# A convolutional row LSTM: the shared third's normalisation on ScalarE, and another order for the half-step

## The chip, the cores and the metric

The kernel runs on one core of a Trainium2 chip. The metric is the device time of one execution in microseconds (us); the time of a kernel is the median of several executions. A core has a matrix engine (TensorE; PE in the profile, with its weight loads as PEld), VectorE (DVE), ScalarE (ACT), GpSimd (POOL), SyncE (SP), which issues the DMAs here, an on-chip memory SBUF and the accumulators PSUM, in which eight banks are used in turn.

## The reference

The input `x` has 8 images of 96 channels and 128 x 128 pixels. It is normalised in 32 groups, and goes through a row LSTM, whose result is added to `x`:

```python
its = conv(X, W_is * mask, 1x3) + b_is        # gates' own input, for all rows
def step(carry, row_in):                      # 128 rows, one after the other
    h, c = carry
    ss = conv(h, W_ss, 3 taps) + b_ss         # 96 -> 384 channels
    gates = ss + row_in                       # f, i, o, g of 32 channels each, three times
    f, i, o, g = sigmoid, sigmoid, sigmoid, tanh
    c_new = f * c + i * g
    h_new = o * tanh(c_new)
    return (h_new, c_new), h_new
x = x + rows(scan(step, groupnorm(x)))
```

Each row needs the state of the row above, so the 128 rows are a chain. The mask of the input's convolution lets the first third of the output channels see the first third of the inputs at the centre tap, the second third two, and the third all.

## The kernel before

**Two chains.** The images are split into two sets of four, s = 0 and s = 1. They share nothing but the weights, so a row of one can be worked while the other waits. A *half-step* is one row of one set; half-step n has row n // 2 of set n % 2, with set 0 one row ahead. There are 256.

**A half-step.** Pixels are held as even and odd ones, 256 of each kind (4 images x 64). The three-tap convolution of a row is taken from four operands, which are made from the new state `hx`: the sum `vs` of even and odd neighbours (S, `total`, L670), their difference `vf` (F, `difference`, L674), and the differences of shifted pixels `te` (D0, `shifted_even`, L680) and `vo` (D1, `shifted_odd`, L684). S and F are VectorE's, D0 and D1 GpSimd's. The products with them are called 1 (`vs`), 2 (`vf`), 0 (`vo`) and 3 (`te`); P, Q and E are those with the row's own input `xs`. Each is made for three tiles A, B and C of 128 gate channels, in one PSUM bank a tile; TensorE works in two lanes of 64 rows, marked `<` and `>`, and all its matmuls are L512.

When a tile's products are there, the two results must be combined: cp (`copy`, L583, ScalarE) brings one half to SBUF, lo (`even`, L587) and hi (`odd`, L591, both VectorE) add and subtract. Then come the gates: ta (tanh, L596), si (sigmoid, L615) and o2 (the last third of the output gate, L618), all on ScalarE; fg (`forget`, f x c, L623, VectorE); gt (i x g, of the odd pixels on VectorE, gtb, L632, of the even on GpSimd, gta, L630); ce (`cell`, L642, VectorE), th (`cell_tanh`, L650, ScalarE), ou (`output`, L658, VectorE, which writes the state `hx`). The letter a or b at a name's end is for the even and odd pixels, a capital for the tile. re (`residual`, L700, VectorE) adds the row to `x`.

**The input's preparation.** The rows are worked in blocks of R = 4, 32 of them. Each half-step also prepares a piece of a later block: W1 (`widen`, L337, GpSimd) normalises 128 x 512 pixels of one image from `xr` to `xw`; W2 (`add_pixels`, L354) and W3 (`subtract_pixels`, L358, both GpSimd) make from it two kinds of operand in `xs`. The channels of the last third, of which there is a copy beside the state (`hx<-x`, 32 partitions), are normalised by `normalise_shared`: mostly in pieces of 32 x 512 or 32 x 384, called U (L337, GpSimd), and once in four rows a piece of 32 x 128, called X (L335, ScalarE). `prepare(n, which)` issues those that `which` names, and with the last of them also the block's DMAs (`load_rows`, `load`, `spare`).

**The order.** The queues are written out by hand. `PERIOD` is a string of names that is issued for each of the half-steps 2 to 253, `LAST` for the end. The order of names within an engine is the order of its queue; between engines only semaphores count. A stroke `'` after a name means the half-step before, `+` the one after; S, F, D0 and D1 count from the row that will use them. So `PERIOD` is a loop over which the steps of several half-steps are spread, and `hiC` to `hiC` is a whole turn. Read by engine, one turn of the string before is:

- VectorE: fg' loB hiB loA gtb' hiA ceb' cea' oub' oua' F' S' loC hiC re'
- ScalarE: siA' cpB siBb' cpA taCb' taCa' siC' o2' thb' X tha' cpC taA siBa
- GpSimd: D0 U W3 D1 W1 gta' W2

Of the kernel before, what the change touches and what calls it, by code (L numbers as in the profile page):

```python
# [21 lines left out]
def kernel(  # L22
# [29 lines left out]
    nc = tc.nc  # L52
# [423 lines left out]
    class HalfStep:  # L476
# [158 lines left out]
        def part(self, ap, lo, hi, t=None):  # L635
            ap = ap.rearrange("p (t b j) -> p t b j", t=2, b=BH)
            return ap[:, :, lo:hi] if t is None else ap[:, t, lo:hi]
# [106 lines left out]
    def work(n):  # L744
        row, s = place(n)
        if row >= NT:
            return [], (), []
        if n < len(FIRST):
            return FIRST[n]
        k, r = divmod(row, R)  # L750
        ahead, image = (k + 2, 0) if r == R - 1 else (k + 1, r + 1)
        return (
            shared(s, k + 1, *SHARED[r]) if k + 1 < NB else [],
            own(s, ahead, image) if ahead < NB else (),
            ([LATER[n]] if n in LATER else [])
            + ([(spare, s, k + 1)] if r == R - 2 and k + 1 < NB else [])
            + ([(load_rows, s, k + 2)] + ([(load, 0, k + 2)] if s == 1 else [])
               if r == R - 2 and k + 2 < NB else []),
        )
# [3 lines left out]
    def prepare(n, which="123"):  # L763

        channels, image, rest = worked.setdefault(n, [list(parts) for parts in work(n)])
        now = []
        for name, engine in (("X", nc.scalar), ("U", nc.gpsimd)):
            if name in which:
                now += [part for part in channels if part[1] is engine]
                channels[:] = [part for part in channels if part[1] is not engine]  # L770
        for i in "123":
            if i in which and int(i) <= len(image) and image[int(i) - 1]:
                now.append(image[int(i) - 1])
                image[int(i) - 1] = None
        if image.count(None) == len(image) and n not in closed:
            closed.add(n)
            now += rest
        for part, *args in now:
            part(*args)
# [3 lines left out]
    def finish(n):  # L783
        prepare(n)
        row, s = place(n)
        k, r = divmod(row, R)
        if r == R - 1:
            store(s, k, R - 1 if k + 1 == NB else 0, R)
            if s == 1 and k + 2 < NB:
                load(s, k + 2)  # L790
        elif r == R - 2 and k + 1 == NB:
            store(s, k, 0, R - 1)
# [2 lines left out]


    PERIOD = (
        "2B> siA' cpB 2A< siBb' 0C'> 1A< cpA fg' D0'' 3C'> QC< loB QA+> taCb' 1C< hiB PB+> 2C< "
# [3 lines left out]
    )  # L802
    LAST = (
        "2B'' 2A'' 1B'' 1A'' cpB'' cpA'' loB'' 1C'' hiB'' 2C'' loA'' EB'' hiA'' 0B'' 3A'' 0A'' "
        "3B'' cpC'' loC'' EA'' taA'' hiC'' 0C'' 3C'' PA QA PB QB PC QC EA EB siBa'' siA'' siBb'' "
        "fg'' taCb'' taCa'' gtb'' siC'' gta'' ceb'' cea'' o2'' thb'' oub'' tha'' oua'' F'' S'' "
        "D1'' D0'' re'' 1A 2A 1B 1C 2B 2C cpA loA hiA cpB loB 3A hiB 0A 0B 3B cpC loC hiC 0C 3C "
        "taA siA fg o2 siBa siBb taCa taCb gta gtb siC ceb cea thb tha oub oua reb rea"
    )
# [17 lines left out]
    def do(n, names, by_lanes=False):  # L827

        for name in names.split():
            if name in "UX":  # L830
                prepare(n - NH, name)
                continue
            if name[0] == "W":
                prepare(n - 1 + name.count("+") - name.count("'"), name.strip("W+'"))
                continue
# [280 lines left out]
    for b in range(B):  # L1116
# [7 lines left out]
        for k in range(QW // CH):  # L1124
# [11 lines left out]
            if alone:  # L1136
                i = list(shares).index(k)
                part = slice(0, alone * SN) if k % 2 else slice(CH - alone * SN, CH)
# [131 lines left out]
```

## Time and profile before

| | |
|---|---|
| median of 3 runs | 2147.67 us (2146.77 to 2148.72) |
| the profiled execution | 2147.14 us |
| its span | 2145.3 us |
| granted TensorE clock | 0.995 |
| busy: PE, PEld | 2044.4 us (95%), 1727.8 us (81%) |
| busy: DVE, ACT, POOL | 1841.4 us (86%), 1584.9 us (74%), 1581.3 us (74%) |
| instructions on DVE, ACT, POOL | 4018, 3519, 1917 |
| U on GpSimd (L337, both shapes) | 245 instructions, 205.8 us |
| X and the like on ScalarE (L335) | 74 instructions, 39.9 us |
| DMA | 242.79 MB, 113 GB/s |

A row of a group (by line, engine, operation and shapes) ends with `| busy us, mean ns of one | idle time of the engine before them`. A row of the chain that ended last has start, length, engine, tile written and line. A row of a timeline has start, length, engine, line, operation, output `<-` inputs, shape, and in brackets the idle time just ahead and what ended it. A row of windows has the stretch, its length, the busy time of PE, PEld, DVE, ACT and POOL, the granted clock, the share of DMA time and GB/s. Times are counted from the start of the span.

### The profile page before, as it was taken

The numbers are of one execution on the slowest core, as the hardware profiler recorded it, in microseconds if no ns is written. First come the engines' busy times: TensorE is split into PE (matmuls) and PEld (weight loads), VectorE is DVE, ScalarE is ACT, GpSimd is POOL, SyncE is SP. The second block draws the span as 40 slices with busy tenths as digits, with TensorE's granted clock in tenths as the row PEclk, the third lists the DMA queues.
The fourth block names the chain that finished last, engine by engine and source line by source line (L and its number), as shares of the span: only waits on it lengthen the run. The fifth ranks groups of instructions, "written<-read, shape, count | busy, mean of one in ns | idle before, by whom it ended". The sixth has DMA issues, their size and how long they took to land.

```text
span 2145.3 us, 45095 instructions
## 1 busy us (share of the span) xinstructions
PE 2044.4 (95%) x16400; PEld 1727.8 (81%) x16400; DVE 1841.4 (86%) x4018; ACT 1584.9 (74%) x3519; POOL 1581.3 (74%) x1917
## 2 busy tenths in 40 slices
PE   3689999999999999999999999999999999999998
PEld 0357888888888888888888888888888888888886
DVE  5788888888888888888888888888888888888887
ACT  6687777777777777777777777777777777777776
POOL 4457877777777777777777777777777777777752
PEclk9989999999999999999999999999999999999999
DMA  9973443343344334334433433443343344334311
GB/s 404 412 222 94 99 109 82 95 114 100 84 102 107 84 95 114 99 83 103 107 83 95 114 98 83 104 107 83 95 114 98 83 105 106 83 95 114 92 35 31
DMA packets 110286, 242.79 MB, mean 113 GB/s; under 512 B 6832, under 2 KB 16368, under 8 KB 104048
## 3 DMA queue, kind: packets, MB, share of 16 engines
q1 hardware_dynamic: 110064, 239.89, 42.0%
q8 instruction: 131, 2.15, 0.4%
q14 instruction: 91, 0.75, 0.1%
HBM read 181.34 MB, written 50.33 MB: 108 GB/s over the span
## 4 chain that ended last, share of the span: by engine, by line
DVE 53%; ACT 21%; PE 18%; issue 4%; DMA 2%; POOL 2%; SPq 0%; DVEq 0%; POOLq 0%; ACTq 0%
PE ps L512 18%; DVE ps L591 12%; DVE ps L587 11%; DVE vs L670 9%; ACT ps L650 7%; DVE c L642 7%; ACT m L583 6%; DVE hx L658 5%; DVE vf L674 5%; DVE g L632 3%; ACT g L596 2%; ACT o L618 2%; DMA xs<-in_x_dram 2%; ACT o L615 2%; ACT hx L335 1%
## 5 line engine op out<-in xcount | busy, mean ns | idle before, releaser
L512 PE MATMUL ps<-vo,wl 64*128 64x256 f32 (+1 forms) x3042 | 815.3, 392 | 27.3 <-DVE ps L591 2.1
L512 PE MATMUL ps<-vs,wm 64*128 64x256 f32 (+1 forms) x3046 | 808.2, 397 | 8.4 <-POOL vs L670 6.0
L512 PE MATMUL ps<-vf,wm 64*128 64x256 f32 (+1 forms) x3046 | 794.9, 385 | 3.2 <-DVE vf L674 1.8
L512 PE MATMUL ps<-te,wl 64*128 64x256 f32 (+1 forms) x3042 | 771.7, 377 | 0.0
L512 PE MATMUL ps<-xs,wx 64*128 64x256 f32 (+1 forms) x3080 | 727.7, 377 | 2.0 <-POOL xs L354 1.8
L512 PEld LDWEIGHTS ps<-xs,wx 64*128 64x128 f32 x3080 | 561.4, 187 | 7.4 <-POOL xs L354 3.4
L512 PEld LDWEIGHTS ps<-vo,wl 64*128 64x128 f32 (+1 forms) x3042 | 421.3, 185 | 163.3 <-DVE ps L591 129.4
L512 PEld LDWEIGHTS ps<-vf,wm 64*128 64x128 f32 (+1 forms) x3046 | 492.7, 186 | 71.5 <-DVE vf L674 29.2
L583 ACT ACTIVATE m<-ps,wl 128x256 f32<-128x256 f32 x766 | 363.1, 474 | 235.1 <-PE ps L512 208.9
L596 ACT ACTIVATE g<-ps 32x512 f32<-32x512 f32 x765 | 317.9, 448 | 254.4 <-PE ps L512 247.9
L512 PEld LDWEIGHTS ps<-te,wl 64*128 64x128 f32 (+1 forms) x3042 | 493.0, 187 | 13.3 <-issue 0.2
L512 PEld LDWEIGHTS ps<-vs,wm 64*128 64x128 f32 (+1 forms) x3046 | 424.9, 186 | 67.3 <-DVE vs L670 40.8
L680 POOL TENSOR_TENSOR te<-hx 96x256 f32<-96x256 f32 x254 | 215.4, 848 | 292.8 <-DVE hx L658 290.8
L587 DVE TENSOR_TENSOR ps<-m,ps 128x256 f32<-128x256 f32 x768 | 324.7, 423 | 82.4 <-ACT m L583 82.0
L358 POOL TENSOR_TENSOR xs<-xw 128x512 f32<-128x512 f32 (+1 forms) x254 | 380.5, 1498 | 20.2
L591 DVE TENSOR_TENSOR ps<-m,ps 128x256 f32<-128x256 f32 x768 | 325.8, 425 | 17.6
L658 DVE TENSOR_TENSOR hx<-o,ps 96x256 f32<-96x256 f32 x512 | 197.4, 415 | 130.0 <-ACT ps L650 129.5
L512 PE MATMUL ps<-xs,wt 64*128 64x256 f32 x1012 | 299.4, 376 | 1.5 <-DVE ps L591 1.5
L630 POOL TENSOR_TENSOR g<-i,g 96x256 f32<-96x256 f32 x251 | 182.6, 727 | 123.9 <-ACT g L596 123.9
L615 ACT ACTIVATE ps<-ps 96x512 f32<-96x512 f32 (+1 forms) x512 | 244.0, 477 | 0.2
L700 DVE TENSOR_TENSOR x<-x,hx 96x512 f32<-96x512 f32 x253 | 232.2, 918 | 0.0
L337 POOL TENSOR_SCALAR hx<-x,rstd,nmr 32x512 f32<-32x512 f32 (+1 forms) x245 | 205.8, 840 | 24.7
(118 smaller groups left out, 2524.4 us busy)
## 6 DMA issues: line engine op xcount, KB each, us to landing
xr<-in_x_dram SPq DMA_DIRECT2D x124, 512.0 KB, 6.4
x<-in_x_dram SPq DMA_DIRECT2D x62, 768.0 KB, 5.9
out_dram<-x SPq DMA_DIRECT2D x62, 768.0 KB, 4.7
xs<-in_x_dram SPq DMA_DIRECT2D x31, 1024.0 KB, 11.2
x<-in_x_dram SPq DMA_DIRECT2D x62, 256.0 KB, 3.2
te<-in_x_dram SPq DMA_DIRECT2D x8, 1024.0 KB, 11.3
hx<-in_x_dram SPq DMA_DIRECT2D x8, 1024.0 KB, 9.7
te<-xs SPq DMA_DIRECT2D x62, 128.0 KB, 2.5
```

The costliest lines, as they stand in the source:

```text
L337: return engine.tensor_scalar(dst, src, scale, shift, ALU.mult, ALU.add)
L358: return engine.tensor_sub(differences, strided(xw[:, 0, :], 0, [(W + 1, n), (J + 1, 2), (1, J)]), strided(xw[:, 0, :], J, [(W + 1, n), (0 ...
L512: made = nc.tensor.matmul(self.ps[a][:, bass.ts(half, HB)][:, cols], weights[rows, bass.ts(a, P)], rhs[rows, cols], start=new, stop=False, ...
L583: nc.scalar.activation(self.m1[a], m1, AF.Identity, bias=column)
L587: nc.vector.tensor_add(self.ps[a][:, 0:HB], self.m1[a], self.ps[a][:, HB:])
L591: nc.vector.tensor_sub(hi, self.m1[a], hi)
L596: nc.scalar.activation(self.part(g, lo, hi, t), self.part(ps, lo, hi, t), AF.Tanh)
L615: nc.scalar.activation(to, gate, AF.Sigmoid)
L658: nc.vector.tensor_mul(self.h[:, t, lo:hi], o, th)
L670: engine.tensor_add(self.operand("vs")[:, 0, lo:hi], e, o)
L680: nc.gpsimd.tensor_sub(to, h[:, :, 1 : J + 1], h[:, :, 0:J])
L700: nc.vector.tensor_add(xo, xo, self.h)
```

## The change

Two things. First, `prepare` now issues both X and U on ScalarE, so U's instruction becomes an activation with scale and bias (L335's form) where it was a multiply and add on GpSimd. Second, both strings are written anew. By engine, one turn of the new `PERIOD` is:

- VectorE: loA hiA loB gtb' hiB ceb' cea' oub' oua' F' S' loC hiC re' fg
- ScalarE: siBb' cpB taCb' taCa' siC' thb' X tha' U cpC siA taA siBa o2 cpA+
- GpSimd: D0 gta' W3 W1+ D1' W2+

Tile A is taken ahead of tile B; gta stands ahead of W3 and W1, D1 behind them, and D0 behind W2; thb stands ahead of cea, and o2 behind the sigmoids of the next gates; the order of the matmuls is other, with the same number of them.

```diff
         for name, engine in (("X", nc.scalar), ("U", nc.gpsimd)):
             if name in which:
-                now += [part for part in channels if part[1] is engine]
+                now += [
+                    (part[0], nc.scalar, *part[2:]) for part in channels if part[1] is engine
+                ]
                 channels[:] = [part for part in channels if part[1] is not engine]
...
     PERIOD = (
-        "2B> siA' cpB 2A< siBb' 0C'> 1A< cpA fg' D0'' 3C'> QC< loB QA+> taCb' 1C< hiB PB+> 2C< "
-        "taCa' loA U gtb' W3 QB+> siC' D1'' EB< 2C> W1+ hiA gta' 0B< 1C> ceb' cea' 3A< 0B> o2' "
-        "thb' 0A< 3B> PA+< oub' X 0A> tha' PC+< cpC oua' F' 3A> S' 3B< loC EA> taA 2B+< W2+ 2A+> "
-        "1B+< hiC 1A+> 0C< 1B+> re' 3C< siBa"
+        "2B> D0'' 0C'< 1C> QA+< loA 2C> hiA siBb' PA+< QB+> 2C< cpB 3A> loB taCb' gtb' hiB QC< "
+        "0A> 1C< taCa' siC' 0B> 0A< 3B> ceb' gta' thb' cea' oub' X 3A< tha' U oua' W3 W1+ EB> F' "
+        "S' cpC D1' PC+< PB++> loC hiC re' 3B< W2+ EA> 0B< siA 2A+> 2B+< 1A+> 1B+< 0C> 2A+< taA "
+        "fg 3C> 1A+< siBa o2 cpA+ 1B+> 3C<"
     )
     LAST = (
-        "2B'' 2A'' 1B'' 1A'' cpB'' cpA'' loB'' 1C'' hiB'' 2C'' loA'' EB'' hiA'' 0B'' 3A'' 0A'' "
-        "3B'' cpC'' loC'' EA'' taA'' hiC'' 0C'' 3C'' PA QA PB QB PC QC EA EB siBa'' siA'' siBb'' "
-        "fg'' taCb'' taCa'' gtb'' siC'' gta'' ceb'' cea'' o2'' thb'' oub'' tha'' oua'' F'' S'' "
+        "2A'' 2B'' 1A'' 1B'' cpA'' 1C'' loA'' 2C'' hiA'' cpB'' 3A'' loB'' hiB'' 0A'' 0B'' 3B'' "
+        "EB'' cpC'' loC'' hiC'' EA'' siA'' 0C'' taA'' fg'' 3C'' PA QA PB QB PC QC EA EB siBa'' "
+        "o2'' siBb'' taCb'' gtb'' taCa'' siC'' ceb'' gta'' thb'' cea'' oub'' tha'' oua'' F'' S'' "
         "D1'' D0'' re'' 1A 2A 1B 1C 2B 2C cpA loA hiA cpB loB 3A hiB 0A 0B 3B cpC loC hiC 0C 3C "
...
```

## The prediction

> **What bounds the kernel now.** I read the page's busy shares first, then the chain that ended last, then one half-step of that chain instruction by instruction, and last the two engines that this change concerns, VectorE (DVE) and GpSimd (POOL), side by side.
>
> ```profile
> span 2145.3 us, 45095 instructions
> PE 2044.4 (95%) x16400; PEld 1727.8 (81%) x16400; DVE 1841.4 (86%) x4018; ACT 1584.9 (74%) x3519; POOL 1581.3 (74%) x1917
> DVE 53%; ACT 21%; PE 18%; issue 4%; DMA 2%; POOL 2%; SPq 0%; DVEq 0%; POOLq 0%; ACTq 0%
> ```
>
> PE is busy 95%, yet the chain holds it for 18%: most of its matmuls are done while something else is awaited. VectorE has 53% of the chain, and GpSimd, from which work is taken, 2%. So what counts is one turn of the loop. A window from one difference F (`vf`, L674) to another 231 turns later (columns: length, then busy time of PE, PEld, DVE, ACT and POOL, clock, DMA share, GB/s):
>
> ```profile
> 238.62:2046.44 1807.82, 1783.50 (x14792) 1535.38 (x14789) 1579.29 (x3465) 1342.27 (x3062) 1412.39 (x1618) 1.00 0.40 98
> ```
>
> 1807.82 / 231 = 7.826 us a half-step. The chain through two of them:
>
> ```profile
> 1007.04 0.44 DVE ps L591
> 1007.52 1.19 PE ps L512 x8
> 1008.73 0.48 ACT m L583
> 1009.24 0.44 DVE ps L587
> ...
> 1011.55 0.43 DVE c L642
> 1011.98 0.68 ACT ps L650 x2
> 1012.72 0.42 DVE hx L658
> 1013.16 0.42 DVE vf L674
> 1013.59 0.75 DVE vs L670
> 1014.34 0.35 DVE ps L587
> 1014.71 0.44 DVE ps L591
> ...
> 1020.05 0.49 ACT hx L335
> ...
> 1022.98 0.44 DVE ps L591
> ```
>
> The loop closes at hiC (L591, tile C): 1007.04 to 1014.71 is 7.67 us, 1014.71 to 1022.98 is 8.27. The longer one holds X, the 32x128 normalisation on ScalarE (ACT), between the two cell tanhs; X comes once in four rows, and (3 x 7.67 + 8.27) / 4 = 7.82 gives the mean. I count t from hiC's start. In the short half-step the copy starts at 1.69, the cell sum of the even pixels (cea, the second L642) at 4.51, F at 6.12, the sum S (L670) at 6.46, loC (L587) at 7.30, hiC at 7.67.
>
> Now S and its neighbours, each as an instruction:
>
> ```profile
> 1013.50 0.83 DVE L670 TENSOR_TENSOR vs<-hx 128x256 f32<-128x256 f32 x1
> 1013.21 0.85 POOL L680 TENSOR_TENSOR te<-hx 96x256 f32<-96x256 f32 x1 [1.01 <-DVE hx L658]
> 1014.16 0.87 POOL L337 TENSOR_SCALAR hx<-x,rstd,nmr 32x512 f32<-32x512 f32 x1
> 164.13 0.42 DVE L674 TENSOR_TENSOR vf<-hx 128x256 f32<-128x256 f32 x1
> 164.26 1.24 POOL L337 TENSOR_SCALAR xw<-xr,rstd,nmr 128x512 f32<-128x512 f32 x1
> 164.47 0.42 DVE L670 TENSOR_TENSOR vs<-hx 128x256 f32<-128x256 f32 x1
> 208.81 0.79 POOL L337 TENSOR_SCALAR xw<-xr,rstd,nmr 128x512 f32<-128x512 f32 x1
> 209.07 1.08 DVE L700 TENSOR_TENSOR x<-x,hx 96x512 f32<-96x512 f32 x1
> ```
>
> S takes 0.42 alone (164.47), 0.83 in the steady loop, while GpSimd's D0 (`te`, L680) runs beside it. The last pair shows why: the residual x, begun 0.26 after the widening W1 (L337 to `xw`), takes 1.08 and ends at 210.15, 0.55 after W1. At 164 it is the other way: W1 starts 0.13 after F, takes 1.24 where 0.79 is enough, and F and S are undisturbed. So a VectorE operation with two SBUF inputs (F, S, the residual) and a GpSimd one run one after the other. In the loop D0 slips in after F (1013.58) and S waits for it: 0.41 us a half-step on the chain. Operations with one PSUM input (L587, L591, L642, L658) show no such lengthening.
>
> **The change, part by part.** (a) *U moves to ScalarE*, the third channel group's normalisation:
>
> ```profile
> L335 ACT ACTIVATE hx<-x,nmr,rstd 32x512 f32<-32x512 f32 x7 | 5.9, 843 | 6.9 <-DVE nmr L329 6.7
> ```
>
> GpSimd loses 0.87, ScalarE gains 0.84 in three half-steps of four. ScalarE was busy 1342.27 / 231 = 5.81 a half-step, so 6.4 to 6.7 of 7.8: it still fits. What stands behind U in its queue is cpC, the copy that loC needs. U runs from tha's end to cpC: cea ends at 4.94, one tanh takes 0.4 by estimate (two, overlapped, 0.68), U ends at 6.2, and cpC (0.48, with 0.03 to the next, by 1008.73 and 1009.24) lets loC start at 6.71. U lies on the path only if loC could start before that. Taken: nothing; the bound is (f)'s short case, where cpC sets loC. U's removal frees S of nothing: U starts at 1014.16, when S is nearly over.
>
> (b) *Tile A ahead of tile B* (copy, loA, hiA first). The same number of half-products lies between hiC and the first copy (four: 0C, 2A, 3C, 1A, before 0C, 1B, 3C, 2B), so the copy stays at 1.69 and loA at 2.20. Cost 0; if the lanes pack worse, one matmul more, 0.1 to 0.2, estimated from the eight in 1.19.
>
> (c) *thb ahead of cea, o2 behind U and the copies.* In the loop before, the two tanhs began together at 1011.98, when both cell sums were done (the even one ends at 1011.98), thb held up behind o2 (L618); now thb can run beside cea, and tha, which came second in the queue, begins when thb did. The even side: cea cannot start before GpSimd's gta has ended. Rows:
>
> ```profile
> 1010.78 0.73 POOL L630 TENSOR_TENSOR g<-i,g 96x256 f32<-96x256 f32 x1 [0.34 <-ACT g L596]
> 1011.47 0.73 POOL L354 TENSOR_TENSOR xs<-xw 128x256 f32<-128x256 f32 x1
> 171.56 0.42 DVE L642 TENSOR_TENSOR c<-ps,g 96x256 f32<-96x256 f32 x1 [1.79 <-POOL g L630]
> 172.89 0.42 DVE L674 TENSOR_TENSOR vf<-hx 128x256 f32<-128x256 f32 x1
> ```
>
> gta runs 3.74 to 4.47, cea starts at 4.51, and from cea to F, where nothing stands between, the second pair takes 1.33. So F can start at 4.51 + 1.33 = 5.84 less rounding; I take 5.82, against 6.12 before: gain 0.30. In a half-step with X, X still stands between thb and tha, and F comes at about 6.3.
>
> (d) *GpSimd's order: from D0 U W3 D1 W1 gta W2 to D0 gta W3 W1 D1 W2.* gta keeps its time, since it waits for ScalarE's tanh. What follows it is new. D1 (`vo`) with W1 now comes after gta, and W3 (L358) and W1 stand in front of F and S:
>
> ```profile
> 159.12 1.16 POOL L358 TENSOR_TENSOR xs<-xw 128x512 f32<-128x512 f32 x1
> 160.38 0.80 POOL L337 TENSOR_SCALAR xw<-xr,rstd,nmr 128x512 f32<-128x512 f32 x1
> ```
>
> From gta's start to the next GpSimd start is 0.69 (1010.78, 1011.47), so W3 starts at 4.44; W3 to W1 is 1.26 (159.12, 160.38), so W1 starts at 5.70 and ends at 6.51. F is ready at 5.82. **W1 is 0.12 ahead.** This is the disputed number. In the rows, W1 0.26 ahead of the residual (208.81, 209.07) makes it wait, W1 0.13 behind F (164.26, 164.13) makes W1 wait. 0.12 lies nearer the middle (0.06) than the first row, on its side; I take it that W1 wins and F waits: F ends 0.28 after W1, as S ends 0.27 after D0 (1014.33, 1014.06), so at 6.79. D1, which needs only the output and has started at about 6.5, slips in as D0 does between F and S in the loop before, and ends 0.46 later, at 7.25 (D0: 1014.06 after F's 1013.58, 0.48). S ends 0.28 after that, at 7.53. Price: S's end moves from 7.29 (1014.33) to 7.53, +0.24, for all half-steps: X's delay of F to 6.3 lies inside W1 and costs nothing any more. hiC came 0.38 after S's end (1014.71, 1014.33): **7.91**.
>
> (e) *D0 and the residual, fg.* D0 comes after W2 and is no longer in S's way: about 8.1 to 8.7. The residual waits for it and ends 0.5 behind it, 9.2; fg, of the same 512 columns, some 0.7 later by estimate (1.08 less the wait of about 0.4), 9.9; the next loA comes at 7.91 + 2.20 = 10.1. Hidden, by 0.2; without the cover, up to 0.5, the delay of the residual.
>
> (f) *PE's order, SP.* Matmuls are as many as before, 1783.50 / 231 = 7.72 busy modelled, but eight of them pass in 1.19, and 64 so would take 9.5 alone while they took 7.67: packing varies, so PE's slack can't be read to better than some tenths. I take 0, as PE's last matmuls wait on S. Bounds: 0 and +0.2. The block loads issued with these steps stand in SP's order only, for blocks two ahead; 0.
>
> *Sum.* 7.91 against 7.826 is +0.084 x 231 = +19.4. The first ten and last nine half-steps have other sizes:
>
> ```profile
> 155.92 1.18 DVE L674 TENSOR_TENSOR vf<-hx 128x256 f32<-128x256 f32 x1
> 2115.51 0.42 DVE L674 TENSOR_TENSOR vf<-hx 128x256 f32<-128x256 f32 x1
> ```
>
> 155.92 to 238.62 is 82.70 for ten; at 7.91, -3.6. 2046.44 to 2115.51 is 69.07 for nine; two of 7.91 and seven without W3 and W1, where D1 stands in S's way as D0 did, only 0.30 earlier (7.37): -1.6. Together +14.2. The profiled execution took 2147.14, 1.84 beyond its span and 0.53 below the median of 2147.67; the difference is added to the median: 2161.9, **2162**.
>
> **The rivals.** *F first (decides below a lead of W1 of about 0.05).* For it: 164.26 shows W1 losing both F and S. Then S starts 0.34 after F and ends at 6.58, cpC sets loC (6.71), hiC comes 0.46 later (1009.24, 1009.70) at 7.17; with X, W1 still wins, 7.91. Mean 7.36: -0.47 x 231 = -109, the ends -9 and -3: 2027. Against it: W1 starts first by (d). The Trainium skill, "SBUF — State Buffer", section "Who interferes with whom", says that the one that issues first gets the shared port pair for the whole instruction and the other blocks. By that rule W1 wins with any lead, my case; but it also says of this rival that W1, issued before S, takes the gap after F. At 164.26 it didn't: S at 164.47 ran in 0.42, so there the trace disagrees.
>
> *W1 takes the gap between F and S.* As D0 does; against it the same row at 164. W1 ends at 6.86, S 7.14, hiC 7.51; with X 7.91; mean 7.61: -50 -7 -2, 2089.
>
> *S passes before D1.* Then S ends at 7.12, hiC at 7.50 (X: 7.62 by cpC); mean 7.53: -68 -8 -2, 2070. Against it: D0 took that gap in the loop before.
>
> *The conflicts vanish.* F 5.82, S at once, cpC the bound: 7.17, with X 7.62, mean 7.28: -126 -10 -3, 2009. Against it are the rows of S.
>
> *D1 goes ahead of the waiting F.* GpSimd's next operation keeps the port from a waiting S in one place:
>
> ```profile
> 206.11 0.85 POOL L680 TENSOR_TENSOR te<-hx 96x256 f32<-96x256 f32 x1 [1.60 <-DVE hx L658]
> 206.92 1.15 POOL L358 TENSOR_TENSOR xs<-xw 128x512 f32<-128x512 f32 x1
> 206.41 1.95 DVE L670 TENSOR_TENSOR vs<-hx 128x256 f32<-128x256 f32 x1
> ```
>
> F would end at 7.4, S at 7.8, hiC at 8.18: +82 -1, 2229. Against it: at 164.47 S passed a GpSimd operation that waited.
>
> *It changes nothing:* a mixture, about one half-step in seven going to F first (0.084 / 0.55), leaves 7.83: 2147.
>
> **How the numbers follow.** Case W1 ahead 0.57, at 2162, its own range 2152 to 2174 (7.88 to 7.95). F first 0.17; gap to W1 0.06; S before D1 0.06; vanishing 0.03; D1 ahead 0.05; mixture 0.06. A measurement of this kernel tells some 0.2%, 4.3 us, from no change. Faster: 0.17 + 0.06 + 0.06 + 0.03 = 0.32; same 0.06; slower 0.62. As the fast cases hold 0.32, the range goes down to the first of them, 2026, and up to 2175.
>
> **What would show it.** Right: all turns alike at 7.9, none of 8.27; F about 0.97 long (5.82 to 6.79), W1 undisturbed at 0.81 and starting 0.1 before F; S near 1.05 with D1 beside it; U 0.84 on ScalarE right behind tha, with cpC's wait hidden; GpSimd idle before gta. Wrong: F of 0.42 with W1 at 1.24; copies later than 1.7; cpC ending after loC could have started; the residual ending after loA's copy is there.

## The result and the profile after

The changed kernel takes 2163.82 us (median of 4 runs, 2162.91 to 2164.83) against 2147.42 for the kernel before on the same chip: the ratio is 1.0076, 95% interval 1.0058 to 1.0093. It is 16 us slower, less than 1%, but the whole interval lies above 1. The page, with the same lines as before:

```profile
span 2161.0 us, 45467 instructions
PE 2053.6 (95%) x16400; PEld 1719.8 (80%) x16400; DVE 1961.4 (91%) x4018; ACT 1816.5 (84%) x3764; POOL 1272.8 (59%) x1672
DVE 63%; PE 16%; ACT 14%; issue 3%; DMA 2%; POOL 1%; ACTq 0%; SPq 0%; DVEq 0%; POOLq 0%
```

GpSimd is busy some 308 us less, ScalarE 232 more, and VectorE, which has exactly as many instructions as before, 120 more. An engine that does the same work in more busy time is being held up inside its instructions. The same holds for a part of GpSimd's 308: U's own time was 205.8 us of it, and most of the rest is waiting that is gone (in the steady loop W3 took 1.52 us in the mean, and takes 1.16 now). The same 231 turns from F to F as a window (length, busy PE, PEld, DVE, ACT, POOL, clock, DMA, GB/s):

```profile
237.17:2064.13 1826.96, 1794.47 (x14792) 1526.68 (x14790) 1696.07 (x3466) 1560.28 (x3293) 1123.01 (x1389) 1.00 0.39 96
```

1826.96 / 231 = 7.909 us a turn, against 7.826. One turn from the chain of work that ended last in this stretch, hiC to hiC:

```profile
1014.27 0.44 DVE ps L591
...
1015.97 0.48 ACT m L583
...
1020.15 0.90 DVE vf L674
1021.05 0.75 DVE vs L670
1021.81 0.35 DVE ps L587
...
1022.18 0.44 DVE ps L591
```

It is 7.91 long. F alone holds the chain for 0.90, where it held it for 0.42. The timelines of VectorE, GpSimd and ScalarE in that turn show what F and S wait for:

```profile
1020.15 0.90 DVE L674 TENSOR_TENSOR vf<-hx 128x256 f32<-128x256 f32 x1
1020.98 0.83 DVE L670 TENSOR_TENSOR vs<-hx 128x256 f32<-128x256 f32 x1
1022.52 1.00 DVE L700 TENSOR_TENSOR x<-x,hx 96x512 f32<-96x512 f32 x1
1024.38 0.43 DVE L587 TENSOR_TENSOR ps<-m,ps 128x256 f32<-128x256 f32 x1 [0.25 <-ACT m L583]
1018.70 1.16 POOL L358 TENSOR_TENSOR xs<-xw 128x512 f32<-128x512 f32 x1
1019.96 0.81 POOL L337 TENSOR_SCALAR xw<-xr,rstd,nmr 128x512 f32<-128x512 f32 x1
1020.75 0.78 POOL L684 TENSOR_TENSOR vo<-hx 128x256 f32<-128x256 f32 x1
1021.49 0.91 POOL L354 TENSOR_TENSOR xs<-xw 128x256 f32<-128x256 f32 x1
1022.36 0.61 POOL L680 TENSOR_TENSOR te<-hx 96x256 f32<-96x256 f32 x1
1019.70 0.84 ACT L335 ACTIVATE hx<-x,nmr,rstd 32x512 f32<-32x512 f32 x1
```

W1 (0.81, undisturbed) ends at 20.77 and F 0.28 later. D1 ends at 21.53 and S 0.28 later. W2, behind D1, takes 0.91 where it took 0.73: it waited for S in its turn. What these VectorE and GpSimd operations share, so that one waits for the other, is called the port from here on. A half-step with X has F later and shorter:

```profile
1028.51 0.44 DVE L674 TENSOR_TENSOR vf<-hx 128x256 f32<-128x256 f32 x1
1028.88 0.83 DVE L670 TENSOR_TENSOR vs<-hx 128x256 f32<-128x256 f32 x1
```

F starts there at 6.33 after hiC (1022.18), nearly all of W1 is over by then, and S stands where it stands in every turn. So X costs nothing, and the 8.27 turns are gone.

### The profile page after: what moved, and what is told of

Same layout as the page of the kernel before. It is cut to its first block, busy times and chain, and to the rows that moved or that the text cites. A ratio compares the mean times of both kernels' runs of the same rounds, so it can differ in the third digit from the quotient of the medians.

```text
span 2161.0 us, 45467 instructions
## 1 busy us (share of the span) xinstructions
PE 2053.6 (95%) x16400; PEld 1719.8 (80%) x16400; DVE 1961.4 (91%) x4018; ACT 1816.5 (84%) x3764; POOL 1272.8 (59%) x1672
## 4 chain that ended last, share of the span: by engine, by line
DVE 63%; PE 16%; ACT 14%; issue 3%; DMA 2%; POOL 1%; ACTq 0%; SPq 0%; DVEq 0%; POOLq 0%
PE ps L512 15%; DVE ps L591 14%; DVE ps L587 13%; DVE vf L674 9%; DVE vs L670 9%; DVE c L642 8%; ACT m L583 6%; ACT ps L650 6%; DVE hx L658 5%; DVE g L632 5%; DMA xs<-in_x_dram 2%; ACT hx L335 2%; DVE bst L1144 1%; DMA te<-in_x_dram 1%; ACT g L596 0%
## 5 line engine op out<-in xcount | busy, mean ns | idle before, releaser
L512 PE MATMUL ps<-te,wl 64*128 64x256 f32 (+1 forms) x3042 | 859.1, 385 | 0.1
L512 PE MATMUL ps<-vs,wm 64*128 64x256 f32 (+1 forms) x3046 | 740.5, 393 | 17.8 <-POOL vs L670 6.4
L512 PEld LDWEIGHTS ps<-vo,wl 64*128 64x128 f32 (+1 forms) x3042 | 528.5, 186 | 145.1 <-DVE ps L591 129.3
L512 PE MATMUL ps<-xs,wx 64*128 64x256 f32 (+1 forms) x3080 | 624.0, 377 | 2.0 <-POOL xs L354 1.8
L512 PEld LDWEIGHTS ps<-vs,wm 64*128 64x128 f32 (+1 forms) x3046 | 458.3, 187 | 133.4 <-DVE vs L670 109.2
L512 PEld LDWEIGHTS ps<-xs,wx 64*128 64x128 f32 x3080 | 454.1, 187 | 7.6 <-POOL xs L354 3.4
L512 PEld LDWEIGHTS ps<-vf,wm 64*128 64x128 f32 (+1 forms) x3046 | 422.3, 185 | 42.5 <-DVE vf L674 5.1
L358 POOL TENSOR_TENSOR xs<-xw 128x512 f32<-128x512 f32 (+1 forms) x254 | 293.4, 1155 | 0.0
L650 ACT ACTIVATE ps<-c 96x256 f32<-96x256 f32 x512 | 196.2, 384 | 87.5 <-DVE c L642 68.4
L335 ACT ACTIVATE hx<-x,nmr,rstd 32x512 f32<-32x512 f32 (+2 forms) x319 | 240.7, 755 | 15.1 <-DVE nmr L329 6.7
```

The lines of the kernel that those rows point to most:

```text
L335: return engine.activation(dst, src, AF.Identity, bias=shift, scale=scale)
L358: return engine.tensor_sub(differences, strided(xw[:, 0, :], 0, [(W + 1, n), (J + 1, 2), (1, J)]), strided(xw[:, 0, :], J, [(W + 1, n), (0 ...
L512: made = nc.tensor.matmul(self.ps[a][:, bass.ts(half, HB)][:, cols], weights[rows, bass.ts(a, P)], rhs[rows, cols], start=new, stop=False, ...
L650: nc.scalar.activation(th, self.part(self.c, lo, hi, t), AF.Tanh)
```

## The experiments

All times are medians; each ratio is to the kernel before, run beside it. A turn is counted from hiC to hiC, and a turn with X is one in which X runs.

**The two parts alone.** First part: the old strings, with U on ScalarE behind tha.

```diff
-taCa' loA U gtb' W3 QB+> ... X 0A> tha' PC+< cpC
+taCa' loA gtb' W3 QB+> ... X 0A> tha' U PC+< cpC
```

> The first part of the change alone: the old order, with U on ScalarE, issued behind tha. Theory (the port: S waits for D0, and U stood behind both): S still 0.83 long beside D0, turns still 7.67 and 8.27, 2147 within 5 us. Rival 1 (taking U from GpSimd frees VectorE's sum): S 0.42, 0.3 to 0.4 us less a half-step, 2050 to 2080. Rival 2 (the load on ScalarE is the price): cpC and the sigmoids come late, 2155 to 2170 as in the whole change.

2375.45, ratio 1.106 (1.104 to 1.107). None of the theories had it. DVE and POOL timelines:

```profile
1011.17 0.42 DVE L674 TENSOR_TENSOR vf<-hx 128x256 f32<-128x256 f32 x1
1011.51 1.95 DVE L670 TENSOR_TENSOR vs<-hx 128x256 f32<-128x256 f32 x1
1011.21 0.85 POOL L680 TENSOR_TENSOR te<-hx 96x256 f32<-96x256 f32 x1 [1.60 <-DVE hx L658]
1012.02 1.15 POOL L358 TENSOR_TENSOR xs<-xw 128x512 f32<-128x512 f32 x1
```

S waits through D0 and then through W3, which follows D0 at once: it ends 0.29 after W3. In the kernel before, U stood between the two, started 0.10 after D0's end, and S came in ahead of U. Taking U away freed no one; it brought W3 up behind D0. The same run shows the other case too: in some turns W3 comes later, and there S is short:

```profile
1047.33 0.84 DVE L670 TENSOR_TENSOR vs<-hx 128x256 f32<-128x256 f32 x1
1047.04 0.85 POOL L680 TENSOR_TENSOR te<-hx 96x256 f32<-96x256 f32 x1 [1.11 <-DVE hx L658]
1048.03 1.17 POOL L358 TENSOR_TENSOR xs<-xw 128x512 f32<-128x512 f32 x1
```

Here W3 starts 0.14 after D0's end. In 143 of the 190 turns of the steady loop W3 starts as D0 ends and S takes 1.95; in the others it starts 0.14 to 0.26 later, or not beside S at all, and S takes 0.83. All S as a group (count: ns min/median/max):

```profile
L670 DVE TENSOR_TENSOR vs<-hx x190: 832/1948/1955, 332.0 to 1985.9; 128x256 f32<-128x256 f32 x190
```

Second part: the new strings, with U on GpSimd behind D0, in the idle stretch.

```diff
-2B> D0'' 0C'< ... tha' U oua' W3 W1+
+2B> D0'' U 0C'< ... tha' oua' W3 W1+
```

> The second part alone: the new order, with U on GpSimd, behind D0, where GpSimd is idle for 2.9 us in the new loop. Theory (the port: F waits for W1, S for D1): no turn changes, 7.91 each, 2164 within 5 us. Rival 1 (ScalarE's 0.84 us more per half-step is the price): 2147 or less. Rival 2 (GpSimd's load matters wherever it lies): slower than 2164 by up to 0.8 us a half-step.

2166.1, ratio 1.0085 (1.0072 to 1.0099); all turns of the steady stretch are 7.9 long. The theory holds: the whole slowdown is the order's, and U's engine makes no difference that can be told in the new order.

**W1 later.** Two memsets of 128x1 on GpSimd between W3 and W1, work that serves nothing.

```diff
-oua' W3 W1+ EB> F'
+oua' W3 Z Z W1+ EB> F'        # Z: nc.gpsimd.memset(pad, 0.0), pad 128x1
```

> The changed kernel with two tiny memsets (some 0.1 us each) on GpSimd between W3 and W1, so that W1 starts 0.0 to 0.1 us behind F in place of 0.19 ahead. Theory (who comes first gets the port, with the turning point near a lead of 0.05): in half-steps without X, F is 0.42 long and S follows at once, W1 is stretched to 1.2 or more, turns of 7.2 to 7.5; with X, F comes later than W1 and waits as before, 8.0 to 8.1. Mean 7.4 to 7.6: 2045 to 2095, although GpSimd has more to do. Rival (no race for a port, GpSimd's work simply takes its time): 2164 or up to 0.2 us a half-step more, 2210.

2096.43, ratio 0.976 (0.974 to 0.978): 67 us less than the changed kernel, with two useless instructions more on the engine, and 1 us above the theory's range. That excludes the rival.

```profile
1013.74 0.42 DVE L675 TENSOR_TENSOR vf<-hx 128x256 f32<-128x256 f32 x1
1014.08 0.89 DVE L671 TENSOR_TENSOR vs<-hx 128x256 f32<-128x256 f32 x1
1013.38 0.25 POOL L834 MEMSET pad<- 128x1 f32 x2
1013.62 1.07 POOL L338 TENSOR_SCALAR xw<-xr,rstd,nmr 128x512 f32<-128x512 f32 x1
```

The memsets moved W1 by only 0.07: it still starts 0.12 ahead of F, and yet F is 0.42 long and W1 is the one that is stretched, to 1.07. With 0.19, W1 had won. So the turning point lies between 0.12 and 0.19, not near 0.05. The memsets ahead of W1 are not what made it lose: in the half-steps of this run and the next that have X, W1 stands behind them too, and with leads of 0.57 and 0.27 it wins. S then waits for W1 (0.89), and turns without X are 7.5, those with X 8.0. With four memsets:

> The changed kernel with four memsets between W3 and W1 in place of the two of the run before (W1 0.12 ahead of F, F first, then W1, then S: turns of 7.49). W1 now starts 0.1 to 0.15 behind F. Theory A (as in the one row of the kernel before where W1 was 0.13 behind F: it loses to S also): S 0.42 after F, turns of 7.2 to 7.4 without X, unless D1 and D0, now later, hold TensorE up; 2045 to 2090. Theory B (a GpSimd operation that waits takes the gap between F and S): S 0.9 to 1.0, turns of 7.5 to 7.7, 2096 to 2130.

2072.4, ratio 0.965 (0.963 to 0.967).

```profile
1024.79 0.42 DVE L675 TENSOR_TENSOR vf<-hx 128x256 f32<-128x256 f32 x1
1025.13 0.42 DVE L671 TENSOR_TENSOR vs<-hx 128x256 f32<-128x256 f32 x1
1024.98 1.17 POOL L338 TENSOR_SCALAR xw<-xr,rstd,nmr 128x512 f32<-128x512 f32 x1
```

W1, 0.19 behind F, loses to S too: theory A. Turns without X are 7.1 to 7.4; those with X, where W1 is 0.27 ahead of F and F takes 0.83, are 8.3.

**What keeps the port.** D1 ahead of F, W1 behind it, and W2 and W3 moved behind D0:

```diff
-2B> D0'' 0C'< ... oua' W3 W1+ EB> F' S' cpC D1' ... re' 3B< W2+ EA>
+2B> D0'' W2 W3 0C'< ... oua' D1' W1+ EB> F' S' cpC ... re' 3B< EA>
```

> The changed kernel with GpSimd's order D0 W2 W3 gta D1 W1: the large W3 and W2 in the idle stretch ahead of gta, D1 (which needs only the odd pixels' output) ahead of F, W1 just behind F's start. Nothing else is changed. Theory (the port): without X, D1 runs from 5.4 to 6.0, F ends at 6.3 to 6.4, S passes W1 and ends at 6.7, cpC and S together let hiC come at 7.2, or 7.45 if the residual, which waits for W1 and D0, delays the next loA; with X, W1 is ahead of F and the turn is 8.1 to 8.2. Mean 7.4 to 7.65, 2045 to 2105. Rival (the turn is set by TensorE or ScalarE at about 7.9): 2155 to 2165.

2460.77, ratio 1.145 (1.144 to 1.147), the worst of all. In half-steps without X, F (0.61) and S (0.41) came as expected; the residual did not:

```profile
1010.85 2.76 DVE L700 TENSOR_TENSOR x<-x,hx 96x512 f32<-96x512 f32 x1
1010.65 0.61 POOL L680 TENSOR_TENSOR te<-hx 96x256 f32<-96x256 f32 x1
1011.22 0.72 POOL L354 TENSOR_TENSOR xs<-xw 128x256 f32<-128x256 f32 x1
1011.90 1.16 POOL L358 TENSOR_TENSOR xs<-xw 128x512 f32<-128x512 f32 x1
```

It waits through D0, W2 and W3 alike, ends 0.55 after W3, and then holds up the next loA. Again D0 is first in the row. In half-steps with X the same three stand beside S, which takes 2.63, and the turn is 11.4 long in place of 8.1 to 8.2:

```profile
1018.93 2.63 DVE L670 TENSOR_TENSOR vs<-hx 128x256 f32<-128x256 f32 x1
```

A memset behind D0, in the first part alone and in this order, and in this order with X moved behind cpC as well:

> The first part alone again (the old order, U on ScalarE behind tha), with one memset of 128x1 on GpSimd between D0 and W3, where U stood. In the run without it S took 1.95 through D0 and W3 and the time was 2375. Theory A (W3 right behind D0 takes the port ahead of the waiting S; U had kept them apart): with the memset S is 0.83 again, turns 7.67 and 8.27, 2147 within 10 us. Theory B (U on ScalarE itself is what cost 228 us): no change, 2370 or more. Theory C (the memset ends too soon to let S in): S near 1.95 or 2.0, 2370 to 2400.

> The order D0 W2 W3 gta D1 W1 with one memset behind D0, all else as in the run without it, where F took 0.6 and S 0.41, as forecast, but the residual waited 2.76 through D0, W2 and W3: 2461. Theory A (what follows right behind D0 keeps the port; a gap lets VectorE in): the residual ends 0.55 after D0, 1.0 to 1.4 long, and does not hold up the next loA; turns 7.2 to 7.4 without X, 8.2 to 8.4 with it (there W1 is ahead of F, and D0 slips in between F and S); 2050 to 2090. Theory B (a queue of GpSimd operations starves the residual with or without a gap): 2400 or more.

> As the run with D1 first and the memset, and X (32x128 on ScalarE, one half-step in four) issued behind cpC and no longer between the two cell tanhs. Theory A: F comes at 5.88 in all half-steps, all turns 7.2 to 7.4, 2000 to 2045. Theory B (a queue of GpSimd operations starves the residual all the same): 2300 or more. Rival (ScalarE or TensorE sets the turn at about 7.5): 2070 to 2080.

2376.42 (1.107, 1.105 to 1.109), 2313.73 (1.078, 1.076 to 1.079) and 2314.65 (1.078, 1.076 to 1.080). In the first, S is 1.98: the memset is over in 0.09 and W3 starts as D0 ends, theory C. So the memset made no gap there. In the second the residual is still 2.8 in 147 of 194 turns; yet the run is 147 us shorter than the one without the memset. About half of that lies in the 47 turns with X, 9.8 in place of 11.4. There S now comes in behind D0 and ahead of W2:

```profile
1029.44 0.94 DVE L671 TENSOR_TENSOR vs<-hx 128x256 f32<-128x256 f32 x1
```

Why the memset helps S here and not in the first run stays open. In the third the residual is 2.8 in every turn: X's place changes which turns are long, and not the time. What sets D0 apart from D1, behind which S came in, is its width, 96 partitions:

```diff
-h, to = self.hx[0:C, 0, lo:hi], self.moving["ve"][0:C, 0]
+h, to = self.hx[0:P, 0, lo:hi], self.moving["ve"][0:P, 0]
```

> The first part alone (2375; S 1.95 through D0 and W3), with D0 over 128 partitions in place of 96: the channels above 96 of its result are then not those of the reference. Theory A (behind an operation on 96 partitions, the next one on 128 keeps the port; behind one on 128 it does not, as S got in behind D1 and ahead of W2 in the changed kernel): S 0.83, turns 7.67 and 8.27, 2147 to 2165. Theory B (W3 behind D0 takes the port whatever D0's width): S 1.95, 2370 to 2380.

2146.36, ratio 0.9994 (0.9983 to 1.0004): 229 us fewer, by 32 partitions more.

```profile
1019.59 0.83 DVE L670 TENSOR_TENSOR vs<-hx 128x256 f32<-128x256 f32 x1
1019.29 0.85 POOL L680 TENSOR_TENSOR te<-hx 128x256 f32<-128x256 f32 x1 [1.60 <-DVE hx L658]
1020.11 1.34 POOL L358 TENSOR_TENSOR xs<-xw 128x512 f32<-128x512 f32 x1
```

W3 still follows at once, but now S goes ahead of it and W3 waits (1.34). With D0 wide, the first part costs and gains nothing that can be told, as the theory of the port had put it for the first run. So D0's width is what decides here. It isn't a rule for every order: in the run with D1 first, W3 went ahead of the waiting residual, and of S, behind W2 also, which has 128 partitions, and D0 was not widened there.

**Other orders.** One name moved in the changed kernel, D1 ahead of W1; then X also behind cpC (from half-step 16 on); then also U back on GpSimd behind D0.

```diff
-oua' W3 W1+ EB> F' S' cpC D1' PC+<
+oua' W3 D1' W1+ EB> F' S' cpC PC+<
```

> The changed kernel with one name moved: D1 ahead of W1 (GpSimd: D0 gta W3 D1 W1 W2). Theory (the port): without X, D1 runs 5.56 to 6.17, F ends at 6.45 (0.6 long), W1, which starts 0.3 behind F, loses to F and S, S ends at 6.85, turns of 7.2 to 7.3; with X, W1 is 0.2 ahead of F and W2 slips in before S, 8.2 to 8.3. Mean 7.45 to 7.55: 2060 to 2080. Rival (the queue's total on GpSimd, unchanged, or ScalarE's load sets the turn): 2155 to 2165.

> The run with D1 ahead of W1, and X issued behind cpC (from half-step 16 on), no longer between the two cell tanhs. Theory (the port): F at 5.88 in every half-step, all turns 7.2 to 7.3: 2005 to 2030. Rival (ScalarE, now at 6.6 of 7.3 us, becomes the bound in the half-steps with X): those at 7.6 to 7.8, 2030 to 2050.

> The same with U back on GpSimd, behind D0, where GpSimd is idle. Theory (U's engine is not what counts): within 0.5% of the run before, 2005 to 2035; at most some 0.05 us a half-step less, as cpC no longer stands behind U. Rival 1 (U's move to ScalarE is needed for the gain: GpSimd's queue delays gta): turns longer by 0.2 or more, 2060 and up. Rival 2 (ScalarE's load holds the turn up): 10 to 30 us less than the run before.

2086.58 (0.971, 0.970 to 0.973), 2036.04 (0.948, 0.946 to 0.950) and **2005.68** (0.934, 0.932 to 0.935). The timelines of the last:

```profile
1012.05 0.59 DVE L674 TENSOR_TENSOR vf<-hx 128x256 f32<-128x256 f32 x1
1012.56 0.41 DVE L670 TENSOR_TENSOR vs<-hx 128x256 f32<-128x256 f32 x1
1011.74 0.61 POOL L684 TENSOR_TENSOR vo<-hx 128x256 f32<-128x256 f32 x1
1012.34 1.24 POOL L337 TENSOR_SCALAR xw<-xr,rstd,nmr 128x512 f32<-128x512 f32 x1
```

D1, started 0.31 ahead of F, costs F 0.17; W1, 0.29 behind F, waits for both. The first came out 7 us above its range: turns without X are 7.1 to 7.4, about as forecast, but those with X are 8.5 and not 8.2 to 8.3; W1 is 0.2 ahead there, F takes 0.90, and S, behind W2, 0.95. In the second the turn behind X is 7.5 to 7.6, and the time lies in the rival's range, not in the theory's. The third run removes it: with U off ScalarE nearly all turns are 7.2 to 7.3. There U's engine does count, 30 us, the upper end of what the rival with ScalarE's load had put, and the theory's 0.5% is exceeded. The chain of the last run:

```profile
PE 87%; DVE 6%; ACT 3%; DMA 3%; POOL 1%; issue 1%; SPq 0%; DVEq 0%; ACTq 0%; POOLq 0%
```

At 7.23 a turn the chain lies on TensorE nearly all the time. That alone doesn't show that TensorE is the bound: it held 86% of the chain in the run before too, from which moving U still took 30 us, and no run gave TensorE less to do.

## Why the prediction was right, and where it was lucky

The forecast was 2162; 2163.82 was measured. Its sum against the trace: 231 steady turns +19.1 (forecast +19.4), the first ten -1.7 (-3.6), the last nine -1.0 (-1.6). The turns without W1 at the end took 7.56, not 7.37: F came some 0.1 later than put, and D1, which started ahead of it there, held it for 0.07 more.

- *(a) U on ScalarE, nothing.* Right here: U takes 0.84 right behind tha, cpC follows at 1020.56, 6.29 after hiC, long before loC. (It comes in every half-step, not in three of four, so ScalarE is busy 6.75 a turn, 1560.28 / 231, and not 6.4 to 6.7; that too was hidden.) But the step named no cover, and there was one: the first part alone costs 228 us. In the new order D0 is followed by GpSimd's idle time, so W3 can't come up behind it.
- *(b), (c).* The copy starts at 1.70, F at 5.88, not 5.82. X costs nothing, as put. F took 0.90, not 0.97, as it began later; S took 0.83, not 1.05, as its record begins only at 6.71, when F is nearly done.
- *(d) W1 ahead of F.* The outcome was right, F's end (forecast 6.79, measured 6.78), D1's (7.25, 7.26) and S's (7.53, 7.54) too. But two terms were mis-sized and cancelled. The lead was 0.19, not 0.12; and the turning point lies between 0.12 and 0.19, not near 0.05. With the lead that it worked with, F would have won, as the run with two memsets shows. That W1 was given the port was right by luck; what follows from it was worked out rightly.
- *(e).* The residual ended at 9.25 (forecast 9.2), loA waited for the copy, not for it: hidden, as put.
- *The rivals.* "F first" was priced at 2027 from one row in which W1 lost F and S. With W1 0.12 ahead of F, S waits for W1, and the price is that of the rival "W1 takes the gap" (7.51 forecast, 7.49 measured); only with W1 behind F does S pass (7.27, not 7.17). "D1 goes ahead of the waiting F" rested on a row that showed D0 followed by W3, which went the other way in the first part alone once D0 was 128 wide; W1, which D1 follows, is 128 wide, and F went ahead of D1.
- *The rule of the Trainium skill* ("SBUF — State Buffer", "Who interferes with whom": the first to issue gets the port for the whole instruction) was weighed as speaking for W1 with any lead. The run with two memsets disagrees: W1 is first by 0.12 in the records, and F runs in 0.42. Being first was enough for D1, a tensor_tensor: in two half-steps of the last run it was 0.01 ahead and F took 0.88. W1, a tensor_scalar, needed a head start.

## What to carry to other kernels

When two engines share something that one holds for a whole instruction, moving work off the engine that isn't the bound can be worth nothing (the new order with U on either engine) or cost much (228 us in the old order), depending on what then follows what: look for which operation stands directly behind the one that is waited for. An engine that has the same instructions and more busy time is waiting inside them, and the cure here was order, not load: one name moved took 77 us off the changed kernel. When most such waits were gone, the balance between engines counted again (30 us for U back on GpSimd), so it has to be measured again then.

## What the runs showed of the hardware

- Behind a GpSimd operation on 96 partitions, a following one on 128 ran ahead of a VectorE operation that had waited longer (S 1.95; the residual 2.76, through two of them); with 128 partitions for the first, VectorE went ahead (S 0.83). The following one did so only where it started as the first ended: with 0.14 to 0.26 between them S was 0.83. A memset on 128x1 between them left S at 1.98 in one order and brought it from 2.63 to 0.94 in another. Behind U, on 32 partitions and 0.10 after D0's end, S came in; whether by U's width or by the 0.10 is not shown. Nor is it shown why width matters, or why W3 kept the residual waiting behind W2, which has 128 partitions.
- W1, a tensor_scalar with scale and shift from SBUF, lost to F with leads of 0.07 to 0.13 (the half-steps without X of the run with two memsets) and won with 0.19 and more in six other runs. D1, a tensor_tensor, won with 0.01.
- A pause of TensorE can cost more than its length. In the first part alone, 11 of some 190 turns, counted from F to F, were 10.1 to 10.5 long; most others with such an S were 8.8 or 9.4. In one of the 11, S's 1.95 left TensorE idle for 1.1 us; the windows on the 3.4 us ahead of the slow stretch, on the pause in them and on what follows:

```profile
1011.00:1014.40 3.40, 2.19 (x15) 0.95 (x12) 3.33 (x6) 2.49 (x5) 3.19 (x4) 1.00 0.00 0
1011.60:1013.50 1.90, 0.80 (x5) 0.37 (x4) 1.90 (x2) 1.85 (x4) 1.90 (x3) 1.00 0.00 0
1014.30:1018.00 3.70, 3.68 (x17) 3.09 (x19) 2.42 (x4) 0.74 (x2) 0.41 (x1) 0.54 0.00 0
```

The granted clock (third column from the end) is 0.54 for the 3.7 us behind it. A matmul there, and one when it was over:

```profile
1015.27 0.63 PE L512 MATMUL ps<-te,wl 64*128 64x256 f32 x1
1018.26 0.38 PE L512 MATMUL ps<-vs,wm 64*128 64x256 f32 x1
```

The Trainium skill, "TensorE: Matmul & The Clock Gate", "Part 1: The HAM clock gate", gives half rate after at least one idle window of some 3.4 us; here TensorE was busy for 2.19 of the 3.4 us ahead of the drop, so an idle time of 1.1 in one piece was enough, though not in most turns with such an S.
